# Attention in query blocks of 464 columns instead of 384

## The chip, the cores and the metric

The kernel runs on one core of one Trainium2 chip. The metric is the device time of one execution, in microseconds. Before the change the median of three runs is 3839.18 us (3835.62 to 3842.34).

## The reference, cut to what matters

The program is four layers on a 48x48x768 image: a ViT block with decomposed relative positions (L0), a Fourier mixer (L1), a scan with diffusion steps (L2), and a second Fourier mixer (L3). The change touches L0's attention alone. There are 12 heads of 64 and T = 48 x 48 = 2304 tokens, each of which is a query and a key:

```python
attn = jnp.einsum('bqc,bkc->bqk', q * scale, k)
rel_h = jnp.einsum('bhwc,hkc->bhwk', r_q, Rh)
rel_w = jnp.einsum('bhwc,wkc->bhwk', r_q, Rw)
attn = (attn.reshape(B * nh, H, W, H, W) + rel_h[:, :, :, :, None] + rel_w[:, :, :, None, :]).reshape(B * nh, H * W, H * W)
attn = jax.nn.softmax(attn, axis=-1)
out = jnp.einsum('bqk,bkc->bqc', attn, v)
```

So every score has a bias that is the sum of a term by the key's row and a term by its column, both depending on the query. After it come the projection, the MLP and the three other layers.

## The kernel before, in words

The program is written with a tile layer: pools hand out buffers, a scheduler puts each engine's instructions into an order when the program is built, and semaphores are set from the tiles' reads and writes. [...] Eight DMA semaphores are used in turn, so a DMA is issued only when the one that last held its semaphore has landed.

**Before attention.** `qkv_phase` makes Q, K, V and the position terms `rw_d` and `rh_d` in DRAM. These tensors keep tokens in three super-blocks of 768 (the index `sb`); within one head the tokens of a super-block are contiguous. Near its end, `load_ahead` (lines 1318 to 1330) opens the pool `at_a` with two query buffers (`qt0`, `qt1`) and two bias buffers (`bt0`, `bt1`) and issues the loads of the first query block, while the last position terms (`relD` loads, L379; `rw` matmuls, L401) are still under way.

**Attention, `attention_bounded`.** It works on pairs of heads (6 pairs, head dimension 64, so that a pair fills 128 partitions), within a pair on query blocks of QB = TB = 384 columns (6 of them), and within a block on 18 key tiles of 128, taken in groups of KB = 3. A unit of `work` is one group: 6 x 6 x 6 = 216 units. For unit i TensorE does

- `products` (L559): for 3 key tiles and 2 heads, K times Q in f32 with 64 rows, into a score tile of two PSUM banks (three such tiles, `at_ps`);
- `scores` (L567): a bf16 matmul that adds the bias, a one-hot matrix of 120 rows times the bias rows `bt`; then ACT takes the exponential into a buffer `p` (L569; ten of them, pool `at_p`), and DVE adds it to the running sum `acc` (L574, L577);
- `values` (L588) for the unit before: V times p in f32, two heads in two column halves, accumulated over the whole block in one PSUM bank `av`.

At a block's end `row_sums` (L595) sums `acc` over partitions by a matmul with ones, DVE takes the reciprocal (L597), and `finish` (L603) multiplies `av` by it into `oT`. There is one `av` bank, so the first `values` of the next block must wait for `finish`.

At a block's first unit the loads of the next block are written down (`load_chunk`, L616 to L620): the queries, and by `load_bias` (L489) for each head two halves of four DMAs in all: 48 rows of column terms (L498) and 72 rows of row terms (L499). Each super-block holds two query blocks of 384, so a block never crosses a super-block.

**Beside it, `weight_sums`.** Sums of weight blocks for the later seven-product matmuls are made on GpSimd while TensorE does attention: 3 parts for the projection, 12 for the first MLP matrix (`left`), 12 for the second (`second`). Each part has three steps (load, combine on GpSimd, store), staggered, so that 29 turns finish them. A turn is taken at each unit with i % 7 == 3 (31 turns). A part borrows one (`left`) or two (`second`) of the ten `p` buffers, by `gate`; ACT's next exponential that gets such a buffer waits for GpSimd (`left`) or for the stores (`second`).

**After it** `proj_phase` runs, whose weight loads (L721) start when attention has ended.

Of the kernel before, what the change touches and what calls it, by code (L numbers as in the profile page):

```python
# [12 lines left out]
F32 = mybir.dt.float32  # L13
BF16 = mybir.dt.bfloat16
AF = mybir.ActivationFunctionType
ALU = mybir.AluOpType
# [4 lines left out]
P = 128  # L21
G = 48
T = G * G
C = 768
NC = C // P
NT = T // P
NH, HD = 12, 64
FF = 4 * C
NF = FF // P
TB = 384  # L30
NTB = T // TB
LN_EPS = 1e-5
KTH, KTW = 8, 16
KJ = G // KTW
NBR = 3 * (KTW + G // 2)
# [450 lines left out]
                advance()  # L486


def load_bias(nc, bt, rw_d, rh_d, h, blk):  # L489

    c, s = divmod(h, 2)
    nw = 3 * KTW
    sb, n = divmod(blk, 2)
    cols = slice((2 * c + n) * TB, (2 * c + n + 1) * TB)
    w = rw_d[s].rearrange("(j k) n b f -> j (k n) b f", j=KJ)[:, :, sb, cols].rearrange("j r t -> r j t")
    r = rh_d[s].rearrange("(a k) n b f -> a (k n) b f", a=2)[:, :, sb, cols]
    for a in range(2):
        nc.sync.dma_start(bt[:nw, a], w)  # L498
        nc.sync.dma_start(bt[nw:NBR, a], r[a].unsqueeze(1).to_broadcast([NBR - nw, KJ, TB]))  # L499


def load_onehot(nc, pool, oneh_d, o):
# [6 lines left out]
def attention_loads(nc, q_d, k_d, v_d, rw_d, rh_d):  # L509

    def keys_values(kv, pr):
        nc.sync.dma_start(kv[:, :T], k_d[pr * P : (pr + 1) * P, :])
        nc.sync.dma_start(kv[:, T:].rearrange("p (t c) -> p t c", t=NT), v_d[:, :, pr * P : (pr + 1) * P])

    def chunk(qb, c):
        pr, qc = c
        nc.sync.dma_start(qb[0], q_d[pr * P : (pr + 1) * P, qc * TB : (qc + 1) * TB])
        for s in range(2):  # L520
            load_bias(nc, qb[1][:, s], rw_d, rh_d, 2 * pr + s, qc)

    return keys_values, chunk


def attention_bounded(tc, ahead, oT, beside, load_next):

    nc = tc.nc
    QB = TB
    KB = 3  # L540
    (load_keys_values, load_chunk), kvs, qbs, ones, oneh = ahead
    with (
        tc.tile_pool(name="at_p", bufs=10) as pp,
        tc.tile_pool(name="at_r", bufs=2) as rp,
        tc.tile_pool(name="at_o", bufs=2) as op,
        tc.tile_pool(name="at_ps", bufs=3, space=PSUM) as ps_s,
        tc.tile_pool(name="at_pv", bufs=1, space=PSUM) as ps_v,
    ):
        keys = [kv[:, :T] for kv in kvs]
        vals = [kv[:, T:].rearrange("p (t c) -> p t c", t=NT) for kv in kvs]  # L550

        probs, scs = {}, {}

        def products(c, kt):
            pr, qc = c
            ps = ps_s.tile([P, 2, 512], F32, tag="s", name=f"s_{pr}_{qc}_{kt}")
            for s in range(2):
                rows = slice(s * HD, (s + 1) * HD)
                nc.tensor.matmul(ps[:, s, :QB], lhsT=keys[pr % 2][rows, kt * P : (kt + 1) * P], rhs=qbs[qc % 2][0][rows], start=True, stop=False)  # L559
            scs[c, kt] = ps  # L560

        def scores(c, kt):
            pr, qc = c
            b, j = divmod(kt, KJ)
            ps = scs.pop((c, kt))
            for s in range(2):
                nc.tensor.matmul(ps[:, s, :QB], lhsT=oneh[:NBR, b % 3, :], rhs=qbs[qc % 2][1][:NBR, s, b // 3, j, :], start=False, stop=True)  # L567
            p = pp.tile([P, 2, QB], F32, tag="p", name=f"p_{pr}_{qc}_{kt}")
            nc.scalar.activation(p, ps[:, :, :QB], AF.Exp)  # L569
            probs[c, kt] = p  # L570

            if kt == 1:
                acc = rp.tile([P, 2, QB], F32, tag="acc", name=f"acc_{pr}_{qc}")
                nc.vector.tensor_tensor(acc, probs[c, 0], p, ALU.add)  # L574
                probs[c] = acc
            elif kt > 1:
                nc.vector.tensor_tensor(probs[c], probs[c], p, ALU.add)  # L577

        avs, recs = {}, {}

        def values(c, kt):
            pr, qc = c
            if kt == 0:
                avs[c] = ps_v.tile([P, 512], F32, tag="av", name=f"av_{pr}_{qc}")
            p = probs.pop((c, kt))
            for s in range(2):
                rows = slice(s * HD, (s + 1) * HD)
                nc.tensor.matmul(avs[c][rows, :QB], lhsT=vals[pr % 2][:, kt, rows], rhs=p[:, s, :], start=kt == 0, stop=kt == NT - 1)  # L588

        def row_sums(c):  # L590
            pr, qc = c
            acc = probs.pop(c)
            rs = ps_v.tile([P, 512], F32, tag="rs", name=f"rs_{pr}_{qc}")
            for s in range(2):
                nc.tensor.matmul(rs[s * HD : (s + 1) * HD, :QB], lhsT=ones, rhs=acc[:, s, :], start=True, stop=True)  # L595
            rec = rp.tile([P, QB], F32, tag="rec", name=f"rec_{pr}_{qc}")
            nc.vector.reciprocal(rec, rs[:, :QB])  # L597
            recs[c] = rec

        def finish(c):  # L600
            pr, qc = c
            av, rec = avs.pop(c), recs.pop(c)
            nc.vector.tensor_tensor(oT[:, pr, qc * QB : (qc + 1) * QB], av[:, :QB], rec, ALU.mult)  # L603

        work = [((pr, qc), k0) for pr in range(NC) for qc in range(T // QB) for k0 in range(0, NT, KB)]
        other = beside(op, lambda name: pp.tile([P, 2, QB], F32, tag="p", name=name))
        for i in range(len(work) + 1):
            if i % 7 == 3:
                next(other, None)
            if i == len(work) - 8:  # L610
                load_next()
            if i < len(work):
                c, k0 = work[i]
                pr, qc = c
                if k0 == 0:
                    nxt = (pr, qc + 1) if qc + 1 < T // QB else (pr + 1, 0)  # L616
                    if nxt[0] < NC:
                        load_chunk(qbs[nxt[1] % 2], nxt)
                    if qc == 1 and pr + 1 < NC:
                        load_keys_values(kvs[(pr + 1) % 2], pr + 1)  # L620
                for kt in range(k0, k0 + KB):
                    products(c, kt)
                for kt in range(k0, k0 + KB):
                    scores(c, kt)
            if i:
                c, k0 = work[i - 1]
                if k0 + KB == NT:
                    row_sums(c)
                for kt in range(k0, k0 + KB):
                    values(c, kt)  # L630
                if k0 + KB == NT:
                    finish(c)
        for _ in other:
            pass


def attention_any(tc, ident, oneh, q_d, k_d, v_d, rw_d, rh_d, oT, beside, load_next):


    nc = tc.nc  # L640
# [6 lines left out]
    with (  # L647
# [8 lines left out]
        ones = cp.tile([1, HD], F32, tag="ones", name="an_ones")  # L656
# [4 lines left out]
        for h in range(NH):  # L661
# [3 lines left out]
            nc.sync.dma_start(qa, q_d[h * HD : (h + 1) * HD, :])  # L665
            bt = hp.tile([P, 2, KJ, T], BF16, tag="bt", name=f"an_bt_{h}")
            for i in range(NTB):
                load_bias(nc, bt[:, :, :, i * TB : (i + 1) * TB], rw_d, rh_d, h, i)
            for t in range(NT):
                s = sp.tile([P, T], F32, tag="s", name=f"an_s_{h}_{t}", bufs=1)  # L670
                m6 = sp.tile([P, T // TB], F32, tag="m6", name=f"an_m_{h}_{t}")
                for i in range(T // TB):
                    ps = ps_s.tile([P, 512], F32, tag="s", name=f"an_sp_{h}_{t}_{i}")
                    cols = slice(i * TB, (i + 1) * TB)
# [12 lines left out]
                for k0 in range(0, NT, 4):  # L687
                    n = min(4, NT - k0)
                    ps = ps_t.tile([P, 512], F32, tag="t", name=f"an_pt_{h}_{t}_{k0}")
                    for j in range(n):  # L690
                        k = k0 + j
                        nc.tensor.transpose(ps[:, j * P : (j + 1) * P], s[:, k * P : (k + 1) * P], ident)
                    ev(pT[:, k0 : k0 + n, col : col + P], ps[:, : n * P].rearrange("p (k q) -> p k q", q=P))
                if t % GQ == GQ - 1:
                    g, n = t // GQ, GQ * P
                    av = ps_v.tile([P, 512], F32, tag="av", name=f"an_av_{h}_{g}")
                    for k in range(NT):
                        nc.tensor.matmul(av[: HD + 1, :n], lhsT=vt[:, k, :], rhs=pT[:, k, :], start=k == 0, stop=k == NT - 1)
                    rec = pp.tile([1, n], F32, tag="rec", name=f"an_rec_{h}_{g}")
                    nc.vector.reciprocal(rec, av[HD : HD + 1, :n])  # L700
                    avs = pp.tile([HD, n], F32, tag="avs", name=f"an_avs_{h}_{g}")
# [590 lines left out]
def block_kernel(ctx: ExitStack, tc: tile.TileContext, a: dict):  # L1292
    nc = tc.nc
# [24 lines left out]
    def load_ahead(stage):  # L1318
        if stage == 0:
            load_onehot(nc, atc, a["oneh"], oneh)  # L1320
            kv_tile()
            loads[0](kvs[0], 0)
            return
        kv_tile()
        pool = at_stack.enter_context(tc.tile_pool(name="at_a", bufs=1, side="left"))
        qbs = [(pool.tile([P, TB], F32, tag=f"qt{i}", name=f"qt{i}"), pool.tile([P, 2, 2, KJ, TB], BF16, tag=f"bt{i}", name=f"bt{i}")) for i in range(2)]
        loads[1](qbs[0], (0, 0))
        ones = pool.tile([P, HD], F32, tag="ones", name="ones")
        nc.vector.memset(ones, 1.0)
        ahead.extend((loads, kvs, qbs, ones, oneh))  # L1330
# [507 lines left out]
```

## Time and profile before

| | |
|---|---|
| median of the runs | 3839.18 us |
| the profiled execution's own time | 3837.04 us |
| its span, first to last instruction | 3835.2 us |
| attention (first L559 to last L588) | 513.8 to 1694.2 us |
| PE busy over the span | 3726.5 us, 97% |
| DVE, ACT, POOL busy | 2058.8, 1146.8, 655.8 us |
| mean granted TensorE clock | 0.987 |
| DMA, mean over the span | 120 GB/s |

In a row of the costliest groups stand the line, the engine and operation, the tiles written and read, the shape, the count, then the busy time in us and the mean ns of one, then the idle time of the engine just before these instructions and what ended most of it. A f32 matmul is recorded as two passes, so L559 has 2592 records for 1296 matmuls. Matmuls are pipelined: the mean of one is longer than the distance between two starts. PEclk is the granted clock, 1.00 being full.

### The profile page before, as it was taken

What the parts mean: (1) busy time and instruction counts of PE and PEld (TensorE: products, weight loads), DVE (VectorE), ACT (ScalarE), POOL (GpSimd) and SP (SyncE); (2) the same over time, 40 slices, a digit from 0 to 9 for tenths busy, and PEclk for the clock granted to TensorE, in tenths of its full rate; (3) what the DMA queues carried; (4) which work ended last, traced back from release to release, by engine and by line L of the source; (5) the groups of instructions that cost most, each with busy time, mean ns of one, the idle gap of its engine ahead of it and who ended that gap; (6) DMA issues with size and microseconds to landing.
All of it is one profiled execution on the core that took longest, in us unless ns stands there. A gap on an engine that the chain in (4) does not pass through costs nothing.

```text
span 3835.2 us, 54419 instructions
## 1 busy us (share of the span) xinstructions
PE 3726.5 (97%) x22018; PEld 2254.6 (59%) x22018; DVE 2058.8 (54%) x3184; ACT 1146.8 (30%) x1911; POOL 655.8 (17%) x498
## 2 busy tenths in 40 slices
PE   8999979999999999999999999999999998999998
PEld 4666544444444444445555555555558876996685
DVE  6655456666666666555524332323325567995455
ACT  1322234444444444420310121012013356223342
POOL 3101001111111111015000000000013310982131
PEclk9999989999999999999999999999999999999999
DMA  7656563333232322124434533443453412112345
GB/s 256 213 188 192 180 186 120 112 105 126 87 114 76 113 77 91 42 71 133 154 107 137 173 104 114 136 146 105 124 160 102 113 41 94 36 36 73 97 116 154
DMA packets 267834, 460.43 MB, mean 120 GB/s; under 512 B 33053, under 2 KB 220373, under 8 KB 261079
## 3 DMA queue, kind: packets, MB, share of 16 engines
q1 hardware_dynamic: 257767, 435.93, 37.2%
q10 hardware_dynamic: 9808, 20.94, 1.5%
q8 instruction: 175, 2.87, 0.3%
q14 instruction: 84, 0.69, 0.1%
HBM read 318.49 MB, written 138.31 MB: 119 GB/s over the span
## 4 chain that ended last, share of the span: by engine, by line
PE 90%; DVE 3%; DMA 2%; POOL 2%; ACT 1%; issue 1%; SPq 0%; ACTq 0%; DVEq 0%; POOLq 0%
PE p L867 13%; PE p L930 13%; PE s L559 12%; PE av L588 12%; PE s L567 6%; PE qk L295 6%; PE c L1094 4%; PE c L1187 3%; PE v L164 3%; PE pj L164 2%; PE f_z L1497 2%; PE f_z L1498 2%; PE f_x L1462 2%; PE so L1272 2%; PE f_u L1512 2%; PE rh L415 1%
## 5 line engine op out<-in xcount | busy, mean ns | idle before, releaser
L577 DVE TENSOR_TENSOR acc<-acc,p 128x768 f32<-128x768 f32 x576 | 583.9, 1014 | 353.9 <-ACT p L569 315.7
L569 ACT ACTIVATE p<-s 128x768 f32<-128x768 f32 x648 | 478.5, 812 | 693.8 <-PE s L567 581.3
L930 PE MATMUL p<-w,h 128*128 128x384 f32 x1512 | 492.7, 486 | 0.0
L559 PE MATMUL s<-qt,kv 64*128 64x384 f32 x2592 | 478.5, 502 | 9.9 <-ACT p L569 7.7
L588 PE MATMUL av<-p,kv 128*64 128x384 f32 x2592 | 464.5, 493 | 0.0
L930 PEld LDWEIGHTS p<-w,h 128*128 128x128 f32 x1512 | 286.2, 190 | 196.9
L559 PEld LDWEIGHTS s<-qt,kv 64*128 64x128 f32 x2592 | 233.1, 187 | 250.6 <-ACT p L569 116.3
L588 PEld LDWEIGHTS av<-p,kv 128*64 128x64 f32 x2592 | 170.0, 136 | 225.2 <-issue 216.1
L867 PE MATMUL p<-x2nT,w 128*128 128x384 f32 x864 | 292.7, 488 | 3.9 <-POOL rr L906 3.9
L295 PE MATMUL qk<-xnT,wqk 128*128 128x384 f32 x756 | 252.4, 491 | 5.2 <-DMA wqk<-wqk_d 5.2
L1187 PE MATMUL c<-H,bands 128*48 128x96 f32 x5632 | 243.8, 247 | 11.1 <-issue 10.9
L567 PE MATMUL s<-bt,oneh 120*128 120x384 bf16 x1296 | 249.2, 329 | 0.0
L1187 PEld LDWEIGHTS c<-H,bands 128*48 128x48 f32 x5632 | 235.6, 124 | 19.5 <-issue 11.3
L867 PEld LDWEIGHTS p<-x2nT,w 128*128 128x128 f32 x864 | 164.8, 191 | 119.2 <-POOL rr L906 4.1
L867 PE MATMUL p<-xT,w 128*128 128x384 f32 x648 | 220.8, 486 | 0.0
L567 PEld LDWEIGHTS <-oneh 120*128 120x128 bf16 x1296 | 109.3, 98 | 174.6 <-issue 116.1
L295 PEld LDWEIGHTS qk<-xnT,wqk 128*128 128x128 f32 x756 | 144.6, 193 | 99.9 <-issue 8.5
L906 POOL TENSOR_TENSOR rr<-rr,ml_b 128x1152 f32<-128x1152 f32 x12 | 31.9, 2660 | 955.6 <-DMA rr<-xr_d 864.4
L862 ACT ACTIVATE h<-h,ml_b 128x384 f32<-128x384 f32 x144 | 88.4, 615 | 345.8 <-DVE h L882 174.3
L1195 POOL TENSOR_TENSOR t<-s,c 128x768 f32<-128x768 f32 x80 | 144.7, 1834 | 178.8 <-DMA bands<-in_bands_dram 169.1
L867 PEld LDWEIGHTS p<-xT,w 128*128 128x128 f32 x648 | 123.1, 190 | 85.9
L597 DVE RECIPROCAL rec<-rs 128x384 f32<-128x384 f32 x36 | 92.1, 2558 | 100.7 <-PE rs L595 100.7
(322 smaller groups left out, 4803.7 us busy)
## 6 DMA issues: line engine op xcount, KB each, us to landing
w<-w1s_d SPq DMA_DIRECT2D x36, 768.0 KB
w<-w2s_d SPq DMA_DIRECT2D x36, 768.0 KB
bt<-rh_d SPq DMA_DIRECT2D x144, 162.0 KB
w<-w1s_d SPq DMA_DIRECT2D x36, 576.0 KB
w<-in_mlp_w_dram SPq DMA_DIRECT2D x27, 768.0 KB
wqk<-wqk_d SPq DMA_DIRECT2D x12, 1344.0 KB
yu<-f_ys SPq DMA_DIRECT2D x24, 672.0 KB
bt<-rw_d SPq DMA_DIRECT2D x144, 108.0 KB
```

What stands on the lines that cost most here:

```text
L164: nc.tensor.matmul(p[:, :TB], lhsT=rhs[n][:, c, t * P : (t + 1) * P], rhs=w[:, c, :], start=c == 0, stop=c == NC2 - 1)
L295: nc.tensor.matmul(p[:, :TB], lhsT=w[:, n, c, :], rhs=ops[sb][n][:, c, :], start=c == 0, stop=c == NC2 - 1)
L559: nc.tensor.matmul(ps[:, s, :QB], lhsT=keys[pr % 2][rows, kt * P : (kt + 1) * P], rhs=qbs[qc % 2][0][rows], start=True, stop=False)
L567: nc.tensor.matmul(ps[:, s, :QB], lhsT=oneh[:NBR, b % 3, :], rhs=qbs[qc % 2][1][:NBR, s, b // 3, j, :], start=False, stop=True)
L569: nc.scalar.activation(p, ps[:, :, :QB], AF.Exp)
L577: nc.vector.tensor_tensor(probs[c], probs[c], p, ALU.add)
L588: nc.tensor.matmul(avs[c][rows, :QB], lhsT=vals[pr % 2][:, kt, rows], rhs=p[:, s, :], start=kt == 0, stop=kt == NT - 1)
L867: nc.tensor.matmul(p[:, :TB], lhsT=w[n][:, c, :], rhs=rhs[n][:, c, :], start=c == 0, stop=c == NC2 - 1)
L930: nc.tensor.matmul(ps[t][:, :TB], lhsT=hs[left, f][:, t * P : (t + 1) * P], rhs=wt[:, f % KW2, :], start=f == 0, stop=f == NF2 - 1)
L1094: nc.tensor.matmul(ps[:K, i, :n], lhsT=v[:, c, tok : tok + K], rhs=w[:, cc, c0 : c0 + n], start=cc == NC - 1, stop=cc == 0)
L1187: nc.tensor.matmul(ps[r0 : r0 + G, k // 4, cols], lhsT=bands[:, n - GC, i, :] if gr else bands0[:, n, i, :], rhs=H[:, n, :, d : d + NPR], ...
L1195: GP.tensor_tensor(t, sc[:, ch], c1[:, m0 : m0 + GC].unsqueeze(2).to_broadcast([P, GC, RR, NPR]), ALU.mult)
```

## The change

The query block becomes QB = 464 columns, so that a pair has NQB = 5 blocks (four of 464, one of 448)[...]. There are 6 x 5 x 6 = 180 units. The two query and bias buffers alternate over all blocks, no longer by the block's number in its pair. `load_bias` takes a first token and a length and splits at super-blocks: block 1 (tokens 464 to 927) is loaded as 304 + 160, block 3 (1392 to 1855) as 144 + 320, the others in one piece. All of attention's tiles of QB columns grow; borrowed `p` buffers are cut to their first 768 elements. A turn of `weight_sums` is taken at each unit with i % 6 == 3 (30 turns).

```diff
+QB = 464
+NQB = -(-T // QB)
...
-def load_bias(nc, bt, rw_d, rh_d, h, blk):
+def load_bias(nc, bt, rw_d, rh_d, h, t0, n):
     c, s = divmod(h, 2)
     nw = 3 * KTW
-    sb, n = divmod(blk, 2)
-    cols = slice((2 * c + n) * TB, (2 * c + n + 1) * TB)
-    w = rw_d[s].rearrange("(j k) n b f -> j (k n) b f", j=KJ)[:, :, sb, cols].rearrange("j r t -> r j t")
-    r = rh_d[s].rearrange("(a k) n b f -> a (k n) b f", a=2)[:, :, sb, cols]
-    for a in range(2):
-        nc.sync.dma_start(bt[:nw, a], w)
-        nc.sync.dma_start(bt[nw:NBR, a], r[a].unsqueeze(1).to_broadcast([NBR - nw, KJ, TB]))
+    at = t0
+    while at < t0 + n:
+        sb, t = divmod(at, 2 * TB)
+        m = min(2 * TB - t, t0 + n - at)
+        cols = slice(2 * c * TB + t, 2 * c * TB + t + m)
+        dst = bt[:, :, :, at - t0 : at - t0 + m]
+        w = rw_d[s].rearrange("(j k) n b f -> j (k n) b f", j=KJ)[:, :, sb, cols].rearrange("j r t -> r j t")
+        r = rh_d[s].rearrange("(a k) n b f -> a (k n) b f", a=2)[:, :, sb, cols]
+        for a in range(2):
+            nc.sync.dma_start(dst[:nw, a], w)
+            nc.sync.dma_start(dst[nw:NBR, a], r[a].unsqueeze(1).to_broadcast([NBR - nw, KJ, m]))
+        at += m
+
+def queries(qc):
+    return slice(qc * QB, min(T, (qc + 1) * QB))
...
-    QB = TB
...
+        size = lambda c: queries(c[1]).stop - queries(c[1]).start
+        held = lambda c: qbs[(c[0] * NQB + c[1]) % 2]
...
-                nc.tensor.matmul(ps[:, s, :QB], lhsT=keys[pr % 2][rows, kt * P : (kt + 1) * P], rhs=qbs[qc % 2][0][rows], start=True, stop=False)
+                nc.tensor.matmul(ps[:, s, :n], lhsT=keys[pr % 2][rows, kt * P : (kt + 1) * P], rhs=held(c)[0][rows, :n], start=True, stop=False)
...
-                nc.tensor.matmul(ps[:, s, :QB], lhsT=oneh[:NBR, b % 3, :], rhs=qbs[qc % 2][1][:NBR, s, b // 3, j, :], start=False, stop=True)
-            p = pp.tile([P, 2, QB], F32, tag="p", name=f"p_{pr}_{qc}_{kt}")
-            nc.scalar.activation(p, ps[:, :, :QB], AF.Exp)
+                nc.tensor.matmul(ps[:, s, :n], lhsT=oneh[:NBR, b % 3, :], rhs=held(c)[1][:NBR, s, b // 3, j, :n], start=False, stop=True)
+            p = pp.tile([P, 2, QB], F32, tag="p", name=f"p_{pr}_{qc}_{kt}")[:, :, :n]
+            nc.scalar.activation(p, ps[:, :, :n], AF.Exp)
...
-        work = [((pr, qc), k0) for pr in range(NC) for qc in range(T // QB) for k0 in range(0, NT, KB)]
-        other = beside(op, lambda name: pp.tile([P, 2, QB], F32, tag="p", name=name))
+        work = [((pr, qc), k0) for pr in range(NC) for qc in range(NQB) for k0 in range(0, NT, KB)]
+        other = beside(op, lambda name: pp.tile([P, 2, QB], F32, tag="p", name=name).rearrange("p a c -> p (a c)")[:, : 2 * TB].rearrange("p (a c) -> p a c", a=2))
         for i in range(len(work) + 1):
-            if i % 7 == 3:
+            if i % 6 == 3:
                 next(other, None)
...
-        qbs = [(pool.tile([P, TB], F32, tag=f"qt{i}", name=f"qt{i}"), pool.tile([P, 2, 2, KJ, TB], BF16, tag=f"bt{i}", name=f"bt{i}")) for i in range(2)]
+        qbs = [(pool.tile([P, QB], F32, tag=f"qt{i}", name=f"qt{i}"), pool.tile([P, 2, 2, KJ, QB], BF16, tag=f"bt{i}", name=f"bt{i}")) for i in range(2)]
```

More of the change, by code (lines that the diff above doesn't have):

```diff
@@ L518, in chunk @@
         pr, qc = c
-        nc.sync.dma_start(qb[0], q_d[pr * P : (pr + 1) * P, qc * TB : (qc + 1) * TB])
+        q = queries(qc)
+        n = q.stop - q.start
+        nc.sync.dma_start(qb[0][:, :n], q_d[pr * P : (pr + 1) * P, q])
         for s in range(2):
-            load_bias(nc, qb[1][:, s], rw_d, rh_d, 2 * pr + s, qc)
+            load_bias(nc, qb[1][:, s, :, :, :n], rw_d, rh_d, 2 * pr + s, q.start, n)
     return keys_values, chunk
@@ L552, in attention_bounded @@
         probs, scs = {}, {}
+        size = lambda c: queries(c[1]).stop - queries(c[1]).start
+        held = lambda c: qbs[(c[0] * NQB + c[1]) % 2]
         def products(c, kt):
             pr, qc = c
+            n = size(c)
             ps = ps_s.tile([P, 2, 512], F32, tag="s", name=f"s_{pr}_{qc}_{kt}")
@@ L563, in scores @@
             pr, qc = c
+            n = size(c)
             b, j = divmod(kt, KJ)
@@ L566, in scores @@
             for s in range(2):
-                nc.tensor.matmul(ps[:, s, :QB], lhsT=oneh[:NBR, b % 3, :], rhs=qbs[qc % 2][1][:NBR, s, b // 3, j, :], start=False, stop=True)
-            p = pp.tile([P, 2, QB], F32, tag="p", name=f"p_{pr}_{qc}_{kt}")
-            nc.scalar.activation(p, ps[:, :, :QB], AF.Exp)
+                nc.tensor.matmul(ps[:, s, :n], lhsT=oneh[:NBR, b % 3, :], rhs=held(c)[1][:NBR, s, b // 3, j, :n], start=False, stop=True)
+            p = pp.tile([P, 2, QB], F32, tag="p", name=f"p_{pr}_{qc}_{kt}")[:, :, :n]
+            nc.scalar.activation(p, ps[:, :, :n], AF.Exp)
             probs[c, kt] = p
             if kt == 1:
-                acc = rp.tile([P, 2, QB], F32, tag="acc", name=f"acc_{pr}_{qc}")
+                acc = rp.tile([P, 2, QB], F32, tag="acc", name=f"acc_{pr}_{qc}")[:, :, :n]
                 nc.vector.tensor_tensor(acc, probs[c, 0], p, ALU.add)
@@ L587, in values @@
                 rows = slice(s * HD, (s + 1) * HD)
-                nc.tensor.matmul(avs[c][rows, :QB], lhsT=vals[pr % 2][:, kt, rows], rhs=p[:, s, :], start=kt == 0, stop=kt == NT - 1)
+                nc.tensor.matmul(avs[c][rows, : size(c)], lhsT=vals[pr % 2][:, kt, rows], rhs=p[:, s, :], start=kt == 0, stop=kt == NT - 1)
         def row_sums(c):
             pr, qc = c
+            n = size(c)
             acc = probs.pop(c)
@@ L594, in row_sums @@
             for s in range(2):
-                nc.tensor.matmul(rs[s * HD : (s + 1) * HD, :QB], lhsT=ones, rhs=acc[:, s, :], start=True, stop=True)
-            rec = rp.tile([P, QB], F32, tag="rec", name=f"rec_{pr}_{qc}")
-            nc.vector.reciprocal(rec, rs[:, :QB])
+                nc.tensor.matmul(rs[s * HD : (s + 1) * HD, :n], lhsT=ones, rhs=acc[:, s, :], start=True, stop=True)
+            rec = rp.tile([P, QB], F32, tag="rec", name=f"rec_{pr}_{qc}")[:, :n]
+            nc.vector.reciprocal(rec, rs[:, :n])
             recs[c] = rec
@@ L602, in finish @@
             av, rec = avs.pop(c), recs.pop(c)
-            nc.vector.tensor_tensor(oT[:, pr, qc * QB : (qc + 1) * QB], av[:, :QB], rec, ALU.mult)
-        work = [((pr, qc), k0) for pr in range(NC) for qc in range(T // QB) for k0 in range(0, NT, KB)]
-        other = beside(op, lambda name: pp.tile([P, 2, QB], F32, tag="p", name=name))
+            nc.vector.tensor_tensor(oT[:, pr, queries(qc)], av[:, : size(c)], rec, ALU.mult)
+        work = [((pr, qc), k0) for pr in range(NC) for qc in range(NQB) for k0 in range(0, NT, KB)]
+        other = beside(op, lambda name: pp.tile([P, 2, QB], F32, tag="p", name=name).rearrange("p a c -> p (a c)")[:, : 2 * TB].rearrange("p (a c) -> p a c", a=2))
         for i in range(len(work) + 1):
-            if i % 7 == 3:
+            if i % 6 == 3:
                 next(other, None)
@@ L615, in attention_bounded @@
                 if k0 == 0:
-                    nxt = (pr, qc + 1) if qc + 1 < T // QB else (pr + 1, 0)
+                    nxt = (pr, qc + 1) if qc + 1 < NQB else (pr + 1, 0)
                     if nxt[0] < NC:
-                        load_chunk(qbs[nxt[1] % 2], nxt)
+                        load_chunk(held(nxt), nxt)
                     if qc == 1 and pr + 1 < NC:
@@ L667, in attention_any @@
             for i in range(NTB):
-                load_bias(nc, bt[:, :, :, i * TB : (i + 1) * TB], rw_d, rh_d, h, i)
+                load_bias(nc, bt[:, :, :, i * TB : (i + 1) * TB], rw_d, rh_d, h, i * TB, TB)
             for t in range(NT):
```

## The prediction

> **What bounds the kernel now.** I read the page's busy shares first, then the costliest groups, then a table of busy time by stretch, and last the order of time around the one gap that table shows.
>
> ```profile
> PE 3726.5 (97%) x22018; PEld 2254.6 (59%) x22018; DVE 2058.8 (54%) x3184; ACT 1146.8 (30%) x1911; POOL 655.8 (17%) x498
> ...
> L577 DVE TENSOR_TENSOR acc<-acc,p 128x768 f32<-128x768 f32 x576 | 583.9, 1014 | 353.9 <-ACT p L569 315.7
> L569 ACT ACTIVATE p<-s 128x768 f32<-128x768 f32 x648 | 478.5, 812 | 693.8 <-PE s L567 581.3
> ...
> L559 PE MATMUL s<-qt,kv 64*128 64x384 f32 x2592 | 478.5, 502 | 9.9 <-ACT p L569 7.7
> L588 PE MATMUL av<-p,kv 128*64 128x384 f32 x2592 | 464.5, 493 | 0.0
> ...
> L567 PE MATMUL s<-bt,oneh 120*128 120x384 bf16 x1296 | 249.2, 329 | 0.0
> ...
> L597 DVE RECIPROCAL rec<-rs 128x384 f32<-128x384 f32 x36 | 92.1, 2558 | 100.7 <-PE rs L595 100.7
> ```
>
> TensorE is the bound, and in attention (513.8 to 1694.2 us) it alone: its three lines sat idle 9.9 us in all, while DVE and ACT waited for each other and for PE. Busy time by stretch, over the parts of one group of three key tiles (products, bias, values), and over the start and the rest of attention:
>
> ```profile
> core 0: us, PE busy (x) PEld busy (x) DVE busy (x) ACT busy (x) POOL busy (x), PEclk, DMA share, GB/s
> 922.86:924.99 2.13, 2.13 (x14) 1.07 (x12) 2.03 (x2) 0.00 (x0) 0.65 (x1) 1.00 0.61 216
> 924.99:926.07 1.08, 1.08 (x8) 0.51 (x6) 0.40 (x1) 0.54 (x1) 0.00 (x0) 1.00 0.94 388
> 926.07:928.16 2.09, 2.09 (x13) 0.77 (x13) 1.68 (x2) 1.68 (x3) 0.00 (x0) 1.00 0.72 297
> 515.00:560.00 45.00, 37.27 (x196) 16.07 (x194) 18.26 (x18) 16.79 (x22) 4.55 (x4) 0.92 0.76 215
> 560.00:1690.00 1130.00, 1130.00 (x6408) 501.12 (x6406) 698.62 (x663) 462.73 (x627) 135.63 (x104) 1.00 0.30 92
> ```
>
> From 560 us on PE is never idle. A group takes 2.13 + 1.08 + 2.09 = 5.30 us, and 5.94 where a block's row sums (0.64) come in. The only hole lies in the first block; in order of time (start, length, what, idle before it):
>
> ```profile
> 543.09 0.43 SPq L757 DMA_DIRECT2D pw0b<-in_proj_w_dram  x1
> ...
> 548.71 0.99 POOL L129 TENSOR_TENSOR pw0p<-pw0b,pw0p 128x384 f32<-128x384 f32 x1 [165.73 <-DMA bt<-rw_d]
> ...
> 550.69 2.21 ACT L569 ACTIVATE p<-s 128x768 f32<-128x768 f32 x3 [10.91 <-POOL pw0p L131]
> ...
> 551.55 4.21 PE L559 MATMUL s<-qt,kv 64*128 64x384 f32 x12 [5.99 <-ACT p L569]
> ```
>
> The sixth group's exponentials need a p buffer that the weight preparation had borrowed (pw0b); its load was issued late, behind everything the SP queue had taken at attention's start, POOL freed it at 550.65, and PE lost 5.99 us, then ran the next products in 4.21 instead of 2.13 and the bias in 2.10 instead of 1.08: another 3.1 us. The release is put down to the bias load, but the tile's own load, issued at 543.09, is what POOL needed.
>
> [...] single bias matmuls of 384 columns start 0.162 to 0.163 us apart [...], and an f32 product, recorded as two passes, has its row-paired passes 0.322 us apart [...]. [...]
>
> **The change, part by part.**
>
> 1. *Fewer, wider groups.* Columns streamed stay the same: 2304 queries per pair. [...] What is left of 5.304 is 0.504 us: [...]. In single starts, the first product pair takes 0.428 instead of 0.322 (+0.105), products to bias +0.096, bias to values +0.10, the first value pair +0.05, values to products +0.10. [...] I take them as independent of n. One width can't prove it; bounds are 0.504 (fixed) and 0.609 (growing with n, so no gain). At 464 a group is then 5.80 + 0.504 = 6.304, at 448 it is 6.104. Row sums grow from 0.641 to 0.775 and 0.748.
>    Before: 36 x (6 x 5.304 + 0.641) = 1168.7. After, per pair: 4 x (6 x 6.304 + 0.775) + 6 x 6.104 + 0.748 = 191.77, times 6 = 1150.6. **Gain 18.1 us**, which is 36 groups of 0.504.
> 2. *ACT and DVE.* An exponential grows by 160 elements at 0.95 ns (the slope from the 480-element PSUM copy's 538 ns to this row's 812) to 0.96 us; 18 of them are 17.3 us of a 38.6 us block. [...] reciprocal 2558 x 464/384 = 3.09, final multiply 0.63: 22.8 us of 38.6. Both hidden behind PE. The tightest join is the next block's first value matmul, which waits for the last multiply in the single av bank: now row sums start at 914.82, the multiply ends 919.78, the matmul starts 920.77, slack 1.0. After: reciprocal from +1.12 to +4.2, one add to +5.3, multiply to +5.9, matmul at 0.78 + 2.5 + 2.5 + 1.3 = +7.1. Slack 1.2; nothing.
> 3. *Bias loads.* Blocks 1 and 3 of each pair cross a boundary of 768 tokens and load in two pieces (304+160, 144+320): 7 pieces per head and pair for 6, so 336 bias DMAs for 288, plus 30 query loads for 36. 42 more issues at some 0.4 us lie on SP, which idles up to 15 us per wait. Packet records give 27 ns at 512 B, 36 at 768, 66 at 1536: by that slope, 1440 packets per piece make 330 us of engine time per pair for 311, over 16 engines 1.2 us in 192, at a mean share of 0.30. [...] Hidden: each block is asked for a whole block (38.6 us) ahead. PE would wait only if landing took that long.
> 4. *Weight preparation every 6 groups.* 30 turns for 31 hold the 29 steps. The borrowed buffer now always comes back at the same place, the block's sixth group or the next first one, two groups after it was asked for. Longest chain: w2 loads issued 1365.7, POOL from 1370.8 to 1376.2, second store issued 1376.3, landed some 3.3 later by my estimate (a 3.3 us store in the chain at 1744.9): 14 us, 16 to 17 where POOL's ops take 1.6. It starts at the third group's bias end; PE would miss it after 2.5 + 12.6 + 3.8 + 2.5 - 1 = 20.4 us. Slack 4 us; nothing.
> 5. *Before and at the start.* The first block's bias loads (eight, plus the query load) stand ahead of the last relD loads, which end the wait at 500.6 to 506.3 in the chain. They carry 265 KB more; at the 240 GB/s of that stretch +1.1 us; I take **+0.7** (0 to 1.5). Then pw0b's place in the SP queue: eight more DMAs and 0.29 MB more ahead of it, +1.3 us [...]. POOL frees at 550.65 + 0.7 + 1.3, p is exponentiated at 552.7 to 553.7, products go on at 553.7. Unhindered PE would get there at 513.8 + 0.7 + 5.7 + 6.5 + 4 x 6.3 = 551.9. So the hole is 1.8 us instead of 5.99, since PE arrives later, [...]: **-4.2 and -3.1**. Bounds: hole as before (0) to no hole (-9.1).
> 6. *After attention* the order of every engine's instructions is unchanged; the last block's tail costs +0.4.
>
> Sum: -18.1 + 0.7 - 7.3 + 0.4 = **-24.3 us**. Against the profiled execution's 3837.0 (3835.2 span and 1.8 around it) that is 3812.7; the median of the runs lies 2.1 above that execution, so **3815**.
>
> **Rivals.** *(A) The start's hole stays*: DMA share is 0.95 there at 530 to 540 us, and if the longer queue delays pw0b by some 6 us instead of 2, only 18.1 - 1 is won: 3822. *(B) The overhead per group grows with columns*: the change then does not do what it says; only the start's 6.2 us are left, 3833. [...] *(C) Borrowed buffers come late in every block* (slower): the 12 w2 steps hold two of ten p buffers until their stores land, now always at the same place, with bias pieces queued between on SP and capped by earlier DMAs' landings. If the chain takes over 20.4 us PE stops. From 22.4 us it costs 2 us in each of 12 blocks and eats the gain; at 23.5 us, 3.1 each, 3852. Against: no stall at any position in 560 to 1690 us before. *(D) Split bias loads land late* in the 12 crossing blocks: 1 us each gives 3827.
>
> **How the numbers follow.** Likeliest case 0.74: 3815, own range 3809 to 3820. A 0.11, B 0.05, D 0.05, C 0.05. The range 3808 to 3824 takes in A and leaves B, C and D and some of the tails. 0.2% (7.7 us) is about what a measurement here can tell from no change: faster 0.91 (likeliest, A, most of D), same 0.05 (B, rest), slower 0.04 (C).
>
> **What would show it.** Products near 2.5 us per group, groups 6.30 apart, blocks 38.6; PE never idle after the first block; hole under 3 us at about 552, and the products after it at full clock; attention ending near 1670. Wrong if PE waits at products for ACT in each block's end (C), bias matmuls wait for bt loads (D), or groups lie 6.4 apart (B).

## The result, and the profile after

The changed kernel takes 3819.3 us (median of 5 runs, 3815.61 to 3820.97) against 3839.18; the ratio is 0.9952 with a 95% interval of 0.9941 to 0.9963. By that ratio it is faster by some 18 us (the two medians lie 19.9 apart), inside the predicted range and 4.3 us above the predicted 3815. The profiled execution took 3815.61 us, 21.4 less than the one before, and is the fastest of the five.

In the lines below PE is TensorE and PEld its weight loads, DVE is VectorE, ACT is ScalarE, POOL is GpSimd, and SPq is the queue that issues DMAs. A hole is a stretch in which TensorE waits; half clock is a granted clock of 0.50. In the changed file the lines are: products L576, bias L585, exponential L587, running sum L595, values L606, row sums L614, reciprocal L616; bias loads L505 and L506, weight loads L776. First the page's busy shares and costliest groups of the kernel after, those that answer to the lines shown of before:

```profile
PE 3707.4 (97%) x20914; PEld 2168.0 (57%) x20914; DVE 2032.0 (53%) x3070; ACT 1135.3 (30%) x1803; POOL 653.5 (17%) x498
...
L595 DVE TENSOR_TENSOR acc<-acc,p 128x928 f32<-128x928 f32 (+1 forms) x480 | 561.6, 1170 | 359.4 <-ACT p L587 328.1
L587 ACT ACTIVATE p<-s 128x928 f32<-128x928 f32 (+1 forms) x540 | 467.9, 940 | 681.5 <-PE s L585 575.1
...
L576 PE MATMUL s<-qt,kv 64*128 64x464 f32 (+1 forms) x2160 | 467.8, 565 | 7.6 <-ACT p L587 5.4
L606 PE MATMUL av<-p,kv 128*64 128x464 f32 (+1 forms) x2160 | 456.3, 557 | 0.0
...
L585 PE MATMUL s<-bt,oneh 120*128 120x464 bf16 (+1 forms) x1080 | 241.3, 359 | 0.0
L616 DVE RECIPROCAL rec<-rs 128x464 f32<-128x464 f32 (+1 forms) x30 | 91.1, 3038 | 98.7 <-PE rs L614 98.7
```

The counts fell by a sixth and the durations rose with the columns. PE's idle time at the products fell from 9.9 to 7.6 us, far less than the 6.0 that a vanished hole would have given; bias and values wait for nothing. Next the order of time on PE in the middle of attention (start, length, what):

```profile
926.05 2.61 PE L576 MATMUL s<-qt,kv 64*128 64x464 f32 x12
928.59 1.35 PE L585 MATMUL s<-bt,oneh 120*128 120x464 bf16 x6
929.87 2.56 PE L606 MATMUL av<-p,kv 128*64 128x464 f32 x12
932.36 2.60 PE L576 MATMUL s<-qt,kv 64*128 64x464 f32 x12
```

From 926.05 to 932.36 a group takes 6.31 us; over all of attention 118 groups of 464 columns lie 6.30 apart, 29 of 448 columns 6.10, and 7.08 (6.96 to 6.98 next to a block of 448) where row sums come in. The table of busy time for the start and for the rest of attention (us; then busy time and records of PE, PEld, DVE, ACT, POOL; granted clock, DMA share, GB/s):

```profile
core 0: us, PE busy (x) PEld busy (x) DVE busy (x) ACT busy (x) POOL busy (x), PEclk, DMA share, GB/s
515.00:560.00 45.00, 39.61 (x182) 14.81 (x182) 19.73 (x17) 18.69 (x22) 4.85 (x4) 0.96 0.78 216
560.00:1667.00 1107.00, 1107.00 (x5314) 415.79 (x5312) 671.14 (x550) 450.51 (x521) 134.33 (x104) 1.00 0.31 93
```

After 560 us PE is again never idle. Before it there is still a hole. Its order of time, with the SP queue's issues that lead to it:

```profile
533.14 0.40 SPq L506 DMA_DIRECT2D bt<-rh_d  x1
...
536.09 8.27 SPq L776 DMA_DIRECT2D pw1p<-in_proj_w_dram  x3
...
544.88 0.43 SPq L776 DMA_DIRECT2D pw0b<-in_proj_w_dram  x1
...
550.67 0.99 POOL L131 TENSOR_TENSOR pw0p<-pw0b,pw0p 128x384 f32<-128x384 f32 x1 [168.65 <-DMA bt<-rw_d]
...
552.64 2.62 ACT L587 ACTIVATE p<-s 128x928 f32<-128x928 f32 x3 [9.57 <-POOL pw0p L133]
...
553.64 4.11 PE L576 MATMUL s<-qt,kv 64*128 64x464 f32 x12 [3.65 <-ACT p L587]
```

POOL freed the borrowed buffer after its second operation, at 552.6; PE waited 3.65 us and ran the next products in 4.11 us in place of 2.6.

Where the 21.8 us of span went, by stage (first product to last value is attention):

| stage | before | after | difference |
|---|---|---|---|
| start of the program to first product | 513.83 | 512.66 | -1.2 |
| attention | 1180.4 | 1158.4 | -22.0 |
| end of attention to end of span | 2141.0 | 2142.3 | +1.3 |

### The profile page after: what moved, and what is told of

Read it like the earlier page. It is cut to its first block, busy times and chain, and to the rows that moved or that the text cites. A ratio compares the mean times of both kernels' runs of the same rounds, so it can differ in the third digit from the quotient of the medians.

```text
span 3813.4 us, 51839 instructions
## 1 busy us (share of the span) xinstructions
PE 3707.4 (97%) x20914; PEld 2168.0 (57%) x20914; DVE 2032.0 (53%) x3070; ACT 1135.3 (30%) x1803; POOL 653.5 (17%) x498
## 4 chain that ended last, share of the span: by engine, by line
PE 87%; DVE 4%; POOL 3%; DMA 3%; ACT 1%; issue 1%; SPq 0%; ACTq 0%; POOLq 0%; DVEq 0%
PE p L886 13%; PE p L949 13%; PE s L576 12%; PE av L606 11%; PE qk L297 6%; PE s L585 6%; PE c L1113 4%; PE v L166 3%; POOL t L1214 2%; PE pj L166 2%; PE f_z L1516 2%; PE f_z L1517 2%; PE f_x L1481 2%; PE so L1291 2%; PE f_u L1531 2%; PE rh L417 1%
## 5 line engine op out<-in xcount | busy, mean ns | idle before, releaser
L595 DVE TENSOR_TENSOR acc<-acc,p 128x928 f32<-128x928 f32 (+1 forms) x480 | 561.6, 1170 | 359.4 <-ACT p L587 328.1
L587 ACT ACTIVATE p<-s 128x928 f32<-128x928 f32 (+1 forms) x540 | 467.9, 940 | 681.5 <-PE s L585 575.1
L576 PE MATMUL s<-qt,kv 64*128 64x464 f32 (+1 forms) x2160 | 467.8, 565 | 7.6 <-ACT p L587 5.4
L606 PE MATMUL av<-p,kv 128*64 128x464 f32 (+1 forms) x2160 | 456.3, 557 | 0.0
L576 PEld LDWEIGHTS s<-qt,kv 64*128 64x128 f32 x2160 | 194.2, 187 | 277.5 <-issue 161.9
L606 PEld LDWEIGHTS av<-p,kv 128*64 128x64 f32 x2160 | 141.9, 136 | 247.1 <-issue 237.8
L1206 PEld LDWEIGHTS c<-H,bands 128*48 128x48 f32 x5632 | 234.8, 123 | 20.6 <-issue 11.3
L585 PE MATMUL s<-bt,oneh 120*128 120x464 bf16 (+1 forms) x1080 | 241.3, 359 | 0.0
L585 PEld LDWEIGHTS <-oneh 120*128 120x128 bf16 x1080 | 90.9, 98 | 190.8 <-issue 110.3
L616 DVE RECIPROCAL rec<-rs 128x464 f32<-128x464 f32 (+1 forms) x30 | 91.1, 3038 | 98.7 <-PE rs L614 98.7
```

Source lines behind the costliest of these rows:

```text
L576: nc.tensor.matmul(ps[:, s, :n], lhsT=keys[pr % 2][rows, kt * P : (kt + 1) * P], rhs=held(c)[0][rows, :n], start=True, stop=False)
L585: nc.tensor.matmul(ps[:, s, :n], lhsT=oneh[:NBR, b % 3, :], rhs=held(c)[1][:NBR, s, b // 3, j, :n], start=False, stop=True)
L587: nc.scalar.activation(p, ps[:, :, :n], AF.Exp)
L606: nc.tensor.matmul(avs[c][rows, : size(c)], lhsT=vals[pr % 2][:, kt, rows], rhs=p[:, s, :], start=kt == 0, stop=kt == NT - 1)
L1206: nc.tensor.matmul(ps[r0 : r0 + G, k // 4, cols], lhsT=bands[:, n - GC, i, :] if gr else bands0[:, n, i, :], rhs=H[:, n, :, d : d + NPR], ...
```

## The experiments

The account to be tested: a group costs its columns plus about half a microsecond that doesn't depend on them, so 36 fewer groups win 18 us; the rest is the first block's hole, which depends on when one weight tile's load comes up in the SP queue. Rivals: the overhead grows with the columns (rival B of the prediction; then nearly all of the gain came from the hole), borrowed buffers come late in every block (C), split bias loads cost time (D), and, new here, the hole comes from crowded DMA engines whatever the queue's order. Eight kernels were run in two sets, each beside runs of the kernel before on the same chip: 3836.43 us (26 runs) in the first set, 3836.94 us (33 runs) in the second.

### Without the first weight turn: both widths with no hole

Leaving out the turn at the fourth group takes the borrowed buffer out of the first block; later turns take its steps. In the changed kernel and in the kernel before:

```diff
-            if i % 6 == 3:
+            if i % 6 == 3 and i > 3:
```

```diff
-            if i % 7 == 3:
+            if i % 7 == 3 and i > 3:
```

> The changed kernel with the weight preparation's first turn at unit 9 instead of 3, so that no p buffer is borrowed in the first block. If the hole at 553.6 us (3.65 us idle and 1.5 us of products and bias at half clock) comes from the borrowed buffer, as step 5 says, PE runs on and the time falls by 5.2 us, 3819.3 to about 3814, and no idle time of PE is left between 520 us and the end of attention. If the hole is a late bias load of the second block or a full DMA queue at the start, it stays, moves to the second block, and the time stays within 1.5 us of 3819.

> The kernel before with the same shift (first turn at unit 10). Step 5 expects its 5.99 us hole and 3.1 us at half clock to go: 3839.2 to about 3830. Between this kernel and the 464-column one with the same shift there is then only the number of groups: 36 x 0.504 = 18.1 us by step 1, less 0.4 for the tail, so groups 5.30 and 6.30 us apart and 17 to 18 us between the two. If part of the gain was in the start, the difference is under 14.

Measured: 3811.64 us (3808.73 to 3811.99, 5 runs; ratio to before 0.9931, 0.9918 to 0.9945) with 464 columns, and 3828.88 us (3824.29 to 3833.07, 14 runs; 0.9979, 0.9971 to 0.9987) with 384. The same table of the first one's start and rest:

```profile
515.00:560.00 45.00, 43.26 (x206) 16.02 (x205) 24.24 (x21) 19.59 (x22) 0.00 (x0) 1.00 0.78 206
560.00:1660.00 1100.00, 1100.00 (x5280) 413.18 (x5279) 664.74 (x546) 448.07 (x518) 135.74 (x108) 1.00 0.31 94
```

PE lost 1.74 us in the first 45 us in place of 5.4, at full clock: the hole is gone, and 1.74 us is what the second group waits in every kernel here. Without a hole attention takes 1171.4 us at 384 columns and 1153.2 at 464. So the width alone is worth 18.2 us by the traces and 17.2 by the medians, the hole was worth 9.0 us of attention at 384 and is worth 5.2 at 464, and the change took only 3.8 us of it. The version with 464 columns and no early turn comes out below both kernels: its ratio to before is 0.9931, for 0.9952 of the changed kernel. The intervals of the two ratios just overlap; the traces show the 5.2 us in attention.

### A narrower block

In the changed kernel, with the early turn left out, seven blocks per pair (six of 336 columns, one of 288), weight turns every eight groups:

```diff
-QB = 464
+QB = 336
...
-            p = pp.tile([P, 2, QB], F32, tag="p", name=f"p_{pr}_{qc}_{kt}")[:, :, :n]
+            p = pp.tile([P, 2, TB], F32, tag="p", name=f"p_{pr}_{qc}_{kt}")[:, :, :n]
...
-        other = beside(op, lambda name: pp.tile([P, 2, QB], F32, tag="p", name=name).rearrange("p a c -> p (a c)")[:, : 2 * TB].rearrange("p (a c) -> p a c", a=2))
+        other = beside(op, lambda name: pp.tile([P, 2, TB], F32, tag="p", name=name))
...
-            if i % 6 == 3:
+            if i % 8 == 3 and i > 3:
```

> The changed kernel with seven blocks a pair (six of 336 columns, one of 288), a turn every 8 units from unit 11 on: the same columns, 252 groups instead of 180. Fixed overhead of 0.504 us per group (step 1): 72 x 0.504 = 36.3 us more than the 464-column kernel with the late first turn, about 3850, and groups of 4.20 + 0.504 = 4.70 us. Overhead that grows with columns (rival B): groups of 4.64 us, no more than 2 us above it, about 3815. If ACT cannot keep up with the shorter groups, PE shows idle time and groups are longer than 4.8.

Measured: 3845.78 us (3840.47 to 3849.01; ratio 1.0022, 1.0014 to 1.003), 34.1 us above the 464 columns without a hole (36.3 by attention alone in the two traces, 1189.6 for 1153.2). On PE, in order of time:

```profile
925.08 1.97 PE L576 MATMUL s<-qt,kv 64*128 64x336 f32 x12
926.98 1.03 PE L585 MATMUL s<-bt,oneh 120*128 120x336 bf16 x6
927.94 1.92 PE L606 MATMUL av<-p,kv 128*64 128x336 f32 x12
929.78 1.97 PE L576 MATMUL s<-qt,kv 64*128 64x336 f32 x12
```

A group takes 4.70 us. From 288 to 464 columns it grows by 2.20 us over 176 columns, which is 12.5 ns per column, the rate behind the 5.80 us that step 1 estimates for 464. Less that, the five widths in these traces leave:

| columns | group distance, us | 12.5 ns x columns | left |
|---|---|---|---|
| 288 | 4.10 | 3.60 | 0.50 |
| 336 | 4.70 | 4.20 | 0.50 |
| 384 | 5.30 | 4.80 | 0.50 |
| 448 | 6.10 | 5.60 | 0.50 |
| 464 | 6.30 | 5.80 | 0.50 |

Between 288 and 464 columns the half microsecond is a constant; 72 more groups of 0.50 are 36 us, and the growing overhead (rival B) is out.

### Values of two groups at once

If the fixed part lies at the changes between products, bias and values, doing values once for two groups should save some of it. In the changed kernel without the early turn, with twelve p buffers:

```diff
-        tc.tile_pool(name="at_p", bufs=10) as pp,
+        tc.tile_pool(name="at_p", bufs=12) as pp,
...
-            if i:
+            if i and i % 2 == 0:
...
-                for kt in range(k0, k0 + KB):
+                for kt in range(k0 - KB, k0 + KB):
                     values(c, kt)
```

> The changed kernel with the late first turn, and values done for two groups at once after every second group (products, bias, products, bias, values of both), with 12 p buffers instead of 10. Two groups then have five changes of form instead of six. If the fixed 0.504 us lies in these changes (0.105 + 0.096 + 0.10 + 0.05 + 0.10 per group; bias to products unknown, taken as 0.10), two groups take about 0.15 us less, 12.46 instead of 12.61, and the whole 13.5 us less: about 3800. If it lies in each group and not in the changes, or if the second products then wait for ACT's exponentials, it is no faster than 3814, with PE idle at products in the second case.

Measured: 3879.86 us (3875.8 to 3882.63; ratio 1.0115, 1.01 to 1.0131): 68 us above the kernel it was made from, a loss that the expectation did not foresee. On PE, in order of time:

```profile
1003.35 1.34 PE L606 MATMUL av<-p,kv 128*64 128x464 f32 x4
1004.61 2.60 PE L576 MATMUL s<-qt,kv 64*128 64x464 f32 x12
1007.15 1.35 PE L585 MATMUL s<-bt,oneh 120*128 120x464 bf16 x6
1008.43 0.99 PE L606 MATMUL av<-p,kv 128*64 128x464 f32 x2
1009.35 2.60 PE L576 MATMUL s<-qt,kv 64*128 64x464 f32 x12
```

The scheduler that orders instructions when the program is built put one values matmul (2 records) in front of the second group's products. That matmul is one head of a key tile. Its other head must then go beside the next key tile's first head, and so on, until the last matmul of the long run is left alone at its end (passes at 1003.74 and 1004.13 with nothing beside them). In the other kernels the two heads of a key tile go through the array's column halves together: their passes start 7 ns apart, and the pair takes 2 x 0.389 us. Apart, each takes that long by itself, 0.78 us more per two groups, and a change to values and back is still made, so none is saved. Two groups take 8.63 + 4.74 = 13.37 us for 12.61: 0.76 x 90 = 68 us, the whole difference. This is no test of what a change of form costs, since the number of changes stayed the same; where inside a group the 0.50 us lies is not shown by it, and rests on the single starts of step 1. What it shows is the price of a broken pair.

### Bias loads split everywhere

The kernel before, each bias load cut into 224 and 160 columns; and the same on the kernel before without the early turn:

```diff
-        nc.sync.dma_start(bt[:nw, a], w)
-        nc.sync.dma_start(bt[nw:NBR, a], r[a].unsqueeze(1).to_broadcast([NBR - nw, KJ, TB]))
+        for x, y in ((0, 224), (224, TB)):
+            nc.sync.dma_start(bt[:nw, a, :, x:y], w[:, :, x:y])
+            nc.sync.dma_start(bt[nw:NBR, a, :, x:y], r[a][:, x:y].unsqueeze(1).to_broadcast([NBR - nw, KJ, y - x]))
```

> The kernel before with every bias load of 384 columns cut into 224 + 160 columns: 576 bias DMAs in place of 288, and runs of 448 and 320 bytes in place of 768. Nothing else is changed. Step 3 (the split is hidden): groups stay 5.30 us apart in all blocks after the first and TensorE has no idle time there; only attention's first block can lose, since the tile that the sixth group waits for is queued behind 8 more DMAs there, and the hole of 5.99 us grows by up to 3 us: 3836 to 3841, where before stands at 3836 to 3839. Rival D (split loads land late): at least 0.3 us in each of 36 blocks, or more than 11 us: above 3848, with bias matmuls idle for bt.

> The same split on the kernel before with the first weight turn left out, which has no hole in the first block and measured 3828.9. Step 3: 3827 to 3832, with no idle time of TensorE in any block. Rival D: above 3840.

Measured: 3836.57 us (3832.54 to 3840.8; ratio to before 1.0001, 0.9993 to 1.001) and 3829.35 us (3822.51 to 3833.47; 0.998, 0.9972 to 0.9988), the same as without the split in both. Of the first, the page's line of the DMA queue (packets, MB, share of 16 engines' span) and the rest of attention:

```profile
q1 hardware_dynamic: 313639, 435.95, 37.6%
560.00:1660.00 1100.00, 1100.00 (x6237) 487.88 (x6237) 680.04 (x644) 451.70 (x612) 135.90 (x104) 1.00 0.32 94
```

The kernel before has on that queue

```profile
q1 hardware_dynamic: 257767, 435.93, 37.2%
```

so there are 55,900 more packets for the same bytes, and PE is never idle. The share is 37.6% in both kernels with every load split; in the three with the kernel before's loads whole it is 37.2, 37.3 and 36.9%, so the split cost between 0.3 and 0.7% of the engines' time. The split is hidden even where every load is split, which is 288 more DMAs and not 48 as in the change. Rival D is out. The hole was expected to grow and didn't: the 8 extra issues hold up the SP queue here too (the weight part's first load, `pw0p`, is issued 20.5 us after attention's first product, for 17.6 before and 20.9 in the changed kernel, which also has the 8 issues but moves more bytes), but in this build the scheduler put the tile's load ahead of another weight part's three loads and not behind them. The hole reads

```profile
550.10 3.64 PE L560 MATMUL s<-qt,kv 64*128 64x384 f32 x12 [5.82 <-ACT p L570]
```

5.82 us for 5.99, and its half clock cost 1.4 us for 3.0.

### Weight turns every six groups, alone

The kernel before with

```diff
-            if i % 7 == 3:
+            if i % 6 == 3:
```

> The kernel before with a weight turn at every sixth group (i % 6 == 3) in place of every seventh, so that a borrowed p buffer always falls on the same place of a block; the first turn stays where it is. Step 4 (slack of some 4 us, less here, since a group is 5.30 us and not 6.30: the window of 20.4 us becomes 17.0 for a chain of 14 to 17 us): no idle time of TensorE after the first block, 3836 to 3839, as before; at the long end of the chain up to 1 us in each of 12 blocks, 3848. Rival C (the buffers come late in every block): 2 us or more in each of 12 blocks, 3860 or more.

Measured: 3836.46 us (3831.95 to 3841.26; ratio 1.0, 0.9991 to 1.0008). Its table of start and rest:

```profile
515.00:560.00 45.00, 39.37 (x200) 17.50 (x200) 20.23 (x20) 16.79 (x22) 4.55 (x4) 0.89 0.78 224
560.00:1660.00 1100.00, 1100.00 (x6238) 487.74 (x6236) 677.78 (x645) 450.68 (x611) 129.51 (x104) 1.00 0.30 94
```

No stall in any block after the first, with a window 3.4 us shorter than the changed kernel's: rival C is out, with room to spare.

### The weight turn ahead of the bias loads

The changed kernel with the turn at a block's first group, where its loads are queued before the next block's bias loads:

```diff
-            if i % 6 == 3:
+            if i % 6 == 0:
```

> The changed kernel with the weight turn at a block's first group (i % 6 == 0) in place of its fourth, so that the weight loads of a turn are queued ahead of the bias loads of the next block and not behind them. If the hole of the first block comes from the place of the tile's load in the SP queue, it is gone here with the turn still taken: no idle time of TensorE at 550 us, and 3811 to 3813, like the kernel that leaves the first turn out (3811.6). Rival: it comes from the crowded DMA engines at attention's start whatever the order; then the hole stays at 2 us or more and the time at 3816 to 3820.

Measured: 3812.33 us (3809.37 to 3814.82; ratio 0.9936, 0.9922 to 0.9949). In order of time:

```profile
524.29 2.15 SPq L776 DMA_DIRECT2D pw0b<-in_proj_w_dram  x1
...
532.19 1.41 POOL L133 TENSOR_TENSOR pw0p<-pw0p,pw0b 128x384 f32<-128x384 f32 x1 [148.29 <-DMA bt<-rh_d]
533.55 1.87 POOL L131 TENSOR_TENSOR pw0p<-pw0b,pw0p 128x384 f32<-128x384 f32 x1
```

```profile
515.00:560.00 45.00, 43.26 (x208) 16.27 (x206) 24.21 (x20) 19.59 (x22) 5.24 (x4) 1.00 0.91 255
```

The turn is taken, its tile's load is issued 20.6 us sooner, POOL is done with it by 535.4, and PE loses only the 1.74 us that all these kernels lose. The DMA engines were busier in this stretch (0.91 for 0.78), so crowding does not make the hole: the place in the queue does. This version and the one without the early turn can't be told apart. Their medians lie 7 to 8 us under the changed kernel's, but the kernel before, run beside them, also read 2.2 to 2.8 us less than beside the changed kernel. What is left is some 5 us, and the traces show 5.2 as the hole and its half clock.

## Why the prediction was right, and where it missed

**Step 1, fewer groups: right.** 6.304 and 6.104 us were predicted, 6.30 and 6.10 measured, and 18.1 us stands against 18.2 between the two hole-free kernels. One width could not prove the fixed 0.504, which was the author's estimate; five widths show it. The starts inside a group agree: the first pair of product passes takes 0.427 us for 0.322 with 384 columns, and 0.493 for 0.389 with 464, 0.104 to 0.105 more in both. Single bias matmuls start 0.196 us apart with 464 columns, for 0.162 to 0.163 with 384.

**Step 2, ACT and DVE hidden: right.** The exponential takes 0.945 us (0.96 estimated), the reciprocal 3.06 (3.09), the add 1.125 in the median of the trace (0.958 with 768 elements before); means are a little longer. DVE was busy 671.1 of the 1107 us after 560 us, or 23.4 of a block's 38.6, for the 22.8 estimated. At one block's end in mid-attention the final multiply ends 948.11 and the next block's first values start at 949.56: slack 1.45, for 1.2.

**Step 3, split loads hidden: right**, and by a wide margin, as the kernel with every load split shows. All loads in runs of 448 and 320 B raised the engines' share from some 37.2% to 37.6%. In the trace after, packets of 320 and 288 B took 20 and 19 ns in the median, which is what the slope of step 3 between 512 and 768 B gives.

**Step 4, weight turns every six: right**; alone it changes nothing.

**Step 5, the start: the mis-sized step.** It held three terms.
The loads of the first block ahead of the last `relD` loads were to cost +0.7. In the SP queue's order of time the kernel before has

```profile
471.30 7.53 SPq L379 DMA_DIRECT2D relD_h<-in_relD_dram  x2
...
500.58 7.78 SPq L379 DMA_DIRECT2D relD_w<-in_relD_dram  x5
```

and the kernel after

```profile
470.21 7.53 SPq L381 DMA_DIRECT2D relD_h<-in_relD_dram  x2
...
499.40 7.47 SPq L381 DMA_DIRECT2D relD_w<-in_relD_dram  x5
```

From one `relD` load to the other it is 29.28 and 29.19 us, and from there to the first product 13.25 and 13.26: the term is zero, its lower bound. Of the 1.2 us by which attention began sooner, 1.1 was there at 470 us, before anything that the change touches; over the ten kernels profiled attention begins anywhere from 510.6 to 514.2, and the three that do identical work up to there (before, and before with either other turn rule) spread over 2.8 us.
The delay of the tile's load was to be +1.3 us, about what its 0.29 MB take at 240 GB/s, the rate from 490 to 500 us before. Measured from the first product, the load is issued 29.3 us on before and 32.2 after. What the eight more DMAs cost was their turn on SP more than their bytes: from 529.90 to 533.54 they are issued one after another, most 0.43 us apart, 3.6 us in all, and in the kernel with every load split the same eight issues, without the bytes, made the next load nearly as late (2.9 us, for 3.3). Step 3 had the price, some 0.4 us an issue; eight of them are 3.2. POOL frees the buffer 3.1 us later than before in that count (39.9 for 36.8), and since PE arrives no later than foreseen (37.3 us after the first product, for 37.4), the hole is 3.65 us where 1.8 was predicted. That the predicted time of 553.7 for the products was met (553.64) is a coincidence of this error and of the earlier start.
The half clock was to vanish with a hole of 1.8 us; this was the author's estimate, and all that the trace before shows for it is a gap of 1.74 us at full clock, ahead of the second group. The hole of 3.65 us brought it back: 1.5 us. All four holes seen in the first block, of 3.65, 3.89, 5.82 and 5.99 us, had half clock. It set in after 2.6 us of one of them, and once after a gap of 1.74 us, as the last section shows. So even the predicted 1.8 us was no sure guard against it.
Together the hole and its half clock gave back 3.8 us where 7.3 were expected.

**Step 6, after attention: +1.3 measured for +0.4, not to be told from scatter.** The same instructions there take from 2139.4 to 2145.9 us over the ten kernels.

**The sum.** -24.3 predicted between the two executions, -21.4 measured; the hole accounts for +3.5 of the difference, and the terms before and after attention, and 0.4 us more outside the span, for the rest, in both directions. That these others nearly cancel is luck. What remains of the 4.3 us is the profiled execution's place among its runs: it lies 3.7 under its median, for 2.1 before.

**The rivals.** A, the hole that stays, was half right: its mechanism (a longer queue delays the load) is what happened, at half its price, 3.1 us and not 6, and the time lies between the forecast and its 3822. B, C and D are each refuted by a kernel of their own.

## What to carry to other kernels

Where TensorE alternates between kinds of matmul in short groups, count the groups: each carried a constant of 0.50 us here, from 288 to 464 columns, and with TensorE the bound, 36 fewer groups won 18.2 us, about 36 times that. Two widths that lie well apart separate the constant from the slope. Price a DMA that something waits for by its place in the issuing queue before its bytes: eight more issues ahead of it, most 0.43 us apart, cost it 3 us here, and the three `pw1p` loads just ahead of it held the queue for 8.27. Moving it ahead of bulk prefetches cost nothing here and won back the whole hole. Where two matmuls share the array by halves, look at the order in which the scheduler has left them: a pair that was separated took twice as long here, 1.56 us for 0.78.

## What the runs showed that was not expected

- The half clock after a hole does not last by the hole's length. Beyond the hole itself the next group and its row sums lost 1.5 us after 3.65, 2.7 after 3.89 (the kernel with turns every six), 1.4 after 5.82 (split loads) and 3.0 after 5.99 (before). The granted clock of the traces tells why: it was 0.50 for 3.41 us in the first and third (from 553.30 and 549.62) and for 6.83 us in the others (from 548.58 and 550.91), always from a moment inside the hole on, and about half of what fell behind the hole was lost. In the traces before and after, each stretch at one clock, the first and last aside, lasts a whole number of steps of 3.41 us, from 1 to 374 of them. In the kernel with turns every six it fell 2.6 us after TensorE had gone idle, in the changed kernel 3.3, in the two others some 5.3. And a gap of 1.74 us, which every kernel here has before its second group, brought half clock in one of the profiles. It is in that of the kernel with turns every six groups, in the same table:

```profile
517.00:519.00 2.00, 1.28 (x4) 0.75 (x6) 0.53 (x1) 2.00 (x3) 0.00 (x0) 0.72 0.95 189
519.00:521.00 2.00, 2.00 (x10) 1.03 (x6) 1.39 (x2) 0.07 (x1) 0.00 (x0) 0.50 1.04 230
```

  Its second group's products took 3.90 us in place of some 2.2. PE had been idle 1.30 us before the first group as well, 3.0 us in all between 511.4 and 517.7; the kernel after, with 2.24 and 1.74 us in the same places, kept full clock, and so did the second group of the eight other kernels, after the same 1.74 us. So one idle length doesn't decide it; what does was not settled.
- Packets of 448 and 320 B in place of 768 cost the DMA engines an estimated 3 to 8 ns for each packet more (0.3 to 0.7% of 16 engines over 3831 us, 180 to 430 us, over 55,900 packets).
- A values matmul of half the array took as long alone as two that run side by side: from one pass to the next it was 0.39 us either way, and two groups took 13.37 us in place of 12.61.
